# A two-layer network on one core: producers and consumers of layer 0 set one turn further apart, and the first entry into layer 1 held until the last scan

## The chip, the cores and the metric

The kernel runs on one core of a Trainium2 chip. The metric is the device time of one execution in microseconds (us), lower being better; the time of a kernel is the median of its runs. Before the change the median of three runs is 2766.09 us, from 2762.88 to 2768.23.

Five engines take part. TensorE (PE) multiplies matrices into PSUM, VectorE (DVE) does elementwise work and scans, ScalarE (ACT) does activations and copies, GpSimd (POOL) does some elementwise work and gathers, and SyncE (SP) issues transfers. Each works through its own instructions in order and waits on semaphores of the others.

## The reference, cut to what matters

The input x has 8 batch entries of 512 tokens of 256 channels, all in fp32. Each of two layers adds an attention-like part and a mixture of experts (MoE) to x, both computed from a layer norm of x. The first layer's attention is a linear recurrence along the tokens, run forwards and backwards:

```python
# layer 0, cut; xn = layernorm(x), per head K = 16 channels
dx  = conv(xn) - xn                                  # taps t-1, t, t+1
xxx = xn + dx * maa_x
m   = tanh(xxx @ maa_w1) projected by maa_w2, five ways
r, k, v, g = (mixed inputs) @ Wr, Wk, Wv, silu(@ Wg)
w_log = -exp(time_decay + tanh(xw @ decay_w1) @ decay_w2)
# forward:  S = exp(w_t) * S + k_t v_t^T ;  y_t  = r_t S
# backward: y_t += r_t S ;  S = exp(w_t) * (S + k_t v_t^T)
y = y * sigmoid(dx @ gate_w + gate_b)
x = x + (groupnorm(y) * ln_w + ln_b) * g @ Wo        # attention
      + sum over top 2 of 8 experts: score * W3(silu(xn W1) * (xn W2))
```

The second layer takes the layer norm of that x and adds a global latent attention followed by a local attention (window of 64), and an MoE with the top 4 of 16 experts and a shared part.

## The kernel before

Layer 0 comes first for all eight entries, then layer 1.

The order on PE, DVE, ACT and SP is the order in which the Python code emits instructions; these queues are pinned. The code is written as generators that yield at the end of a step. `Turns.turn()` advances every running generator by one step. So a `yield` in a generator is a distance of one turn in every pinned queue: what follows it stands behind whatever the other generators emit in that turn. This is the whole schedule: which engine waits for which is set by how many turns lie between a producer and its consumer.

`scans` sets the pace. It has 128 items, 8 entries b by 2 halves of the channels c by 8 groups of value channels vg, and each item has four turns. In the first turn DVE multiplies a tile kv by the keys (`L884`), and SP issues the eight transfers that fetch the next item's kv (`spread`, `L861`) into one of four buffers. Turns two and three each hold a pair of scans over the 512 tokens (`L895`, `L899`). In the fourth DVE multiplies by r (`L904`). What PE has to add up from the finished kv tiles (`sums`, `L910`) is kept in a list `late`, and emitted for two items at a time in the first turn of every second item. One entry b is thus 16 items or 64 turns.

Beside `scans`, these generators run:

- `projections(b + 1)` makes the next entry's inputs in three generators. `inputs` makes dx and xxx on DVE (`L748`, `L753`) and their projection t on PE (`L761`). `values` makes the gate, the values v, which go through memory (`vd`, `L782`) to `spread`, and the keys. `decays` makes the decay d (ACT, `L815`), q (DVE, `L819`), `near` (ACT, `L827`) and dq (DVE, `L831`). Its mixed inputs xf come from matmuls m (`L720`) and DVE (`L727`).
- `ending(b, c, ...)` follows the last sums of a half: gate yg (DVE, `L930`), centering yc (PE, `L933`), square and copy (ACT), variance (PE, `L943`), its root (ACT) and reciprocal (DVE, `L951`), widening (ACT, `L954`), transposes rs (PE, `L959`), scaling z (DVE, `L961`), and after the second half the output projection o (PE, `L973`), added to x on DVE (`L978`) and stored to `after`.
- `experts` works through 39 chunks of 256 token slots of the MoE in 12 turns each: a transposed input xsT (PE into PSUM, copied by ACT at `L598`), matmuls g and u (`L606`), silu, products h on DVE (`L615`), matmuls y (`L645`), and a store to `outs`.

After the last chunk, `last` starts `begin`. It loads layer 1's weights from ACT's queue and starts `entry(0)`, which gathers the experts' rows of entry 0 (POOL, `L286`), accumulates them on DVE (`L294`), normalizes, transposes and routes for layer 1.

PSUM banks are shared by tags; `rs` and `var` have the tag `rw`, whose two banks also serve some of the projections.

Of the kernel before, what the change touches and what calls it, by code (L numbers as in the profile page):

```python
# [26 lines left out]
F32 = mybir.dt.float32  # L27
I32 = mybir.dt.int32
AF = mybir.ActivationFunctionType
ALU = mybir.AluOpType  # L30
# [6 lines left out]
P = 128  # L37
B, T, D = 8, 512, 256
NC = D // P
NT = T // P  # L40
# [7 lines left out]
CH = 256  # L48
NS = CH // P
TOP0 = 2  # L50
NCH = B * T * TOP0 // CH + E0 - 1
# [114 lines left out]
def two_layers(ctx: ExitStack, tc: tile.TileContext, a: dict, out: bass.AP):  # L166
# [97 lines left out]
    done = set()  # L264

    def until(*what):
        while what not in done:
            yield
# [4 lines left out]
    def entry(b):  # L273
# [5 lines left out]
        nc.sync.dma_start(acc, tokens(after[b]))  # L279
        for half in range(2):  # L280
            ys = []
            for t in range(2 * half, 2 * half + 2):
                n = b * NT + t
                for i in range(2):
                    y = temp([P, D], "y0", f"y0_{n}_{i}", 4)
                    pool_e.indirect_dma_start(  # L286
                        out=y, out_offset=None, in_=outs,
                        in_offset=bass.IndirectOffsetOnAxis(ap=slot[i][:, n : n + 1], axis=0),
                    )
                    ys.append((t, n, i, y))  # L290
            yield
            yield
            for t, n, i, y in ys:
                vec_e.scalar_tensor_tensor(  # L294
                    acc[:, t, :], y, wslot[i][:, n : n + 1], acc[:, t, :], ALU.mult, ALU.add
                )
        yield
# [14 lines left out]
        ps = bank(f"lg_{b}")  # L312
# [54 lines left out]
    with ExitStack() as l0:  # L367
# [219 lines left out]
        def experts():  # L587
            nxt = weights(0, "wgu", a["w0_gu"], GU0, 2)
            xs = load_slots(0)
            for _ in range(3):  # L590
                yield
            ps = turned(0, xs)
            yield
            for i in range(NCH):
                w, xps = nxt, ps
                wd = weights(i, "wdn", a["w0_dn"], DN0, 1)
                xT = ex.tile([P, NC, CH], F32, tag="xT", name=f"xsT_{i}", bufs=1)
                act_e.copy(xT, xps)  # L598
                if i + 1 < NCH:
                    nxt = weights(i + 1, "wgu", a["w0_gu"], GU0, 2)  # L600
                    xs = load_slots(i + 1)
                yield

# [17 lines left out]
                for j in range(3):  # L621
                    g = ps_gu.tile([P, 2, CH], F32, tag="gu", name=f"g_{i}_{j}")
                    hidden(g[:, 0, :], 4 * j * D)
                    hidden(g[:, 1, :], (4 * j + 2) * D)
                    yield
                    if last:
                        product(j - 1, *last)
                    u = ps_gu.tile([P, 2, CH], F32, tag="gu", name=f"u_{i}_{j}")
                    n = 2 - j // 2
                    for k in range(n):  # L630
                        hidden(u[:, k, :], (4 * j + 2 * k + 1) * D)
                    act_e.activation(hs[j][:, :n, :], g[:, :n, :], AF.Silu)  # L632
                    if n == 1:
                        act_e.activation(hs[j][64:, 1, :], g[:64, 1, :], AF.Silu)
                    last = g, u
                    yield
                if i + 1 < NCH:
                    ps = turned(i + 1, xs)
                product(2, *last)
                yield  # L640
                y = ps_gu.tile([P, NS, D], F32, tag="gu", name=f"y_{i}")
                for n in range(NS):
                    for j in range(NJ0 + 1):
                        lo = 64 * (j == NJ0)
                        pe.matmul(  # L645
                            y[:, n, :], hs[j // 2][lo:, j % 2, n * P : (n + 1) * P],
                            wd[lo:, j * D : (j + 1) * D], start=j == 0, stop=j == NJ0,
                        )
                        if j % 3 == 2:
                            yield  # L650
                ys = ex.tile([P, NS, D], F32, tag="ys", name=f"ys_{i}", bufs=1)
                act_e.copy(ys, y)
# [7 lines left out]
        def projections(b):  # L660
# [75 lines left out]
            def inputs():  # L736
# [7 lines left out]
                for c in range(NC):  # L744
                    o = dx[:, c, :]
                    vec_e.tensor_scalar(o, xT[c], V("conv1", c), None, ALU.mult)
                    for s, n in ((-1, "conv0"), (1, "conv2")):
                        vec_e.scalar_tensor_tensor(o, shifted(c, s), V(n, c), o, ALU.mult, ALU.add)  # L748
                    yield
                xxx = []  # L750
                for c in range(NC):
                    t = mix(f"xxx{c}", c)
                    vec_e.scalar_tensor_tensor(t, dxs[c], V("maa_x", c), xT[c], ALU.mult, ALU.add)  # L753
                    xxx.append(t)
                yield
                both = ((t5a, 0, 0, P), (t5b, P, 64, 96))
# [35 lines left out]
            def decays():  # L792
# [22 lines left out]
                act_e.activation(dT, dT, AF.Exp, scale=-1.0)  # L815
                yield

# [8 lines left out]
                for c in range(NC):  # L826
                    act_e.activation(near[c], near[c], AF.Exp, scale=-1.0)  # L827
                yield
                dq = big("dq")
# [40 lines left out]
        def scans(turns):  # L870
# [4 lines left out]
            for n, (b, c, vg) in enumerate(todo):  # L875
# [8 lines left out]
                vec_e.tensor_tensor(kv, kv, bc(kc, 1, NV), ALU.mult)  # L884
                if len(late) == 2:
                    for sums in late:
                        sums()
                    late = []
                if vg == 0:
                    y = ps_s.tile([P, T], F32, tag="ys", name=f"ys{c}_{b}")  # L890
                if n + 1 < len(todo) and ("keys", todo[n + 1][0]) in done:
                    kvs[todo[n + 1]] = spread(*todo[n + 1])
                yield
                for i in range(NV):
                    vec_e.tensor_tensor_scan(  # L895
                        out=kv[:, i, :], data0=qc, data1=kv[:, i, :], initial=0.0,
                        op0=ALU.mult, op1=ALU.add,
                    )
                    vec_e.tensor_tensor_scan(  # L899
                        out=kv[:, i, ::-1], data0=dc[:, ::-1], data1=kv[:, i, ::-1],  # L900
                        initial=0.0, op0=ALU.mult, op1=ALU.add,
                    )
                    yield
                vec_e.tensor_tensor(kv, kv, bc(rc, 1, NV), ALU.mult)  # L904
# [12 lines left out]
                late.append(sums)  # L917
                yield
            for sums in late:
                sums()  # L920

        def ending(b, c, y, z, x):
# [7 lines left out]
            vec_e.tensor_tensor(yg, sig[:, c, :], y, ALU.mult)  # L930
            yield
            yc = ps_e.tile([P, T], F32, tag="e", name=f"yc{c}_{b}")
            pe.matmul(yc, C["center"], yg, start=True, stop=True)  # L933
# [3 lines left out]
            zc = z[:, c, :]  # L937
            act_e.copy(zc, yc)
            yield

# [13 lines left out]
            act_e.copy(wide, bc(sd, 2, HD))  # L954
            yield
            rs = ps_rw.tile([P, T], F32, tag="rw", name=f"rs{c}_{b}")
            for t in range(NT):
                cols = slice(t * P, (t + 1) * P)
                pe.transpose(rs[:, cols], wide[:, t, :, :].rearrange("p v h -> p (v h)"), ident)  # L959
            yield  # L960
            vec_e.tensor_tensor(zc, zc, rs, ALU.mult)  # L961
# [34 lines left out]
        def begin():  # L996
# [16 lines left out]
            turns.add(entry(0))  # L1013
            for _ in range(6):
                yield
            for name, of, shape in (
# [504 lines left out]
```

## Time and profile before

| | |
|---|---|
| median of 3 runs | 2766.09 us (2762.88 to 2768.23) |
| the profiled execution | 2771.45 us |
| its span in the profile | 2769.7 us |
| mean granted TensorE clock | 0.914 |
| PE busy | 2380.8 us, 86% |
| DVE busy | 2151.8 us, 78% |
| ACT busy | 882.4 us, 32% |
| POOL busy | 500.1 us, 18% |
| memory read, written | 215.22 MB, 31.46 MB |

The span is the time from the first to the last record of the profiled execution; its own time is 1.75 us longer. Busy shares are means over both layers and hide that their limits differ: layer 0 fills about the first 1500 us and layer 1 the rest. The views used below are the windows (busy time of every engine in stretches of time, with the granted PE clock), the waits (for each pair of a waiting line and the line it waited for: total, times, longest), and the groups of instructions by line (busy time, mean ns of one, idle time before them and what ended it).

### The profile page before, as it was taken

How to read it: one execution, taken by the hardware profiler on the slowest of the kernel's cores; microseconds unless marked ns; L12 is line 12 of the kernel's file. 1: busy time of each engine (PE TensorE's matmuls, PEld its weight loads, DVE VectorE, ACT ScalarE, POOL GpSimd, SP SyncE). 2: the span in 40 equal slices, each digit the busy share in tenths (PEclk: the TensorE clock that was granted, in tenths of full speed). 3: DMA queues.
4: the chain of work that ended last, by engine and by line, in shares of the span. 5: the costliest groups of instructions: out<-in, count | busy, mean ns of one | idle time of the engine just before them, and what ended most of it. 6: DMA issues, size and time to landing. Idle time of an engine off the chain costs nothing.

```text
span 2769.7 us, 32796 instructions
## 1 busy us (share of the span) xinstructions
PE 2380.8 (86%) x11900; PEld 1420.3 (51%) x11900; DVE 2151.8 (78%) x3063; ACT 882.4 (32%) x1684; POOL 500.1 (18%) x441
## 2 busy tenths in 40 slices
PE   6697998988989889798844899998989989998996
PEld 4354555545555555555622444555545545555554
DVE  7799989898898999989985766566676675656656
ACT  1232231222322223132111244434343433434344
POOL 2133222322323223232122100001010101001000
PEclk9689989999999899999965999999999999999998
DMA  6335445454454544554542100001011110000000
GB/s 220 106 97 151 140 132 173 141 147 131 146 155 149 149 149 141 158 151 135 157 137 85 45 22 24 12 24 29 19 32 31 31 31 29 24 22 26 20 9 16
DMA packets 100832, 248.87 MB, mean 90 GB/s; under 512 B 24992, under 2 KB 50368, under 8 KB 95552
## 3 DMA queue, kind: packets, MB, share of 16 engines
q1 hardware_dynamic: 70528, 113.32, 14.9%
q0 software_dynamic: 21168, 115.75, 13.2%
q10 hardware_dynamic: 8976, 17.69, 1.8%
q8 instruction: 96, 1.57, 0.2%
q14 instruction: 64, 0.52, 0.1%
HBM read 215.22 MB, written 31.46 MB: 89 GB/s over the span
## 4 chain that ended last, share of the span: by engine, by line
PE 55%; DVE 28%; issue 7%; DMA 4%; ACT 3%; SPq 2%; POOL 1%; DVEq 0%; ACTq 0%; POOLq 0%
PE y L1404 6%; PE g L1358 5%; PE u L1358 4%; DVE kv L895 4%; PE g L606 4%; PE y L645 4%; PE u L606 3%; DVE kv L899 3%; PE sc_g L1256 2%; DMA kv<-vd 2%; PE o_g L1284 2%; DVE kv L884 2%; PE ys L910 2%; PE t L761 2%; PE qkv_l L1148 2%
## 5 line engine op out<-in xcount | busy, mean ns | idle before, releaser
L899 DVE TENSOR_TENSOR_SCAN kv<-d,kv 128x512 f32<-128x512 f32 x256 | 336.5, 1314 | 8.8
L895 DVE TENSOR_TENSOR_SCAN kv<-dq,kv 128x512 f32<-128x512 f32 x256 | 321.6, 1256 | 2.6
L645 PE MATMUL y<-wdn,h 128*128 128x256 f32 x936 | 261.8, 419 | 12.1 <-DVE h L615 11.3
L606 PE MATMUL g<-xsT,wgu 128*128 128x256 f32 x936 | 236.7, 398 | 27.9 <-ACT xsT L598 24.2
L1264 ACT ACTIVATE pt_g<-sc_g 128x512 f32<-128x512 f32 (+1 forms) x384 | 171.0, 531 | 274.8 <-PE sc_g L1256 228.1
L645 PEld LDWEIGHTS y<-wdn,h 128*128 128x128 f32 x936 | 176.7, 203 | 112.8 <-issue 70.0
L606 PEld LDWEIGHTS g<-xsT,wgu 128*128 128x128 f32 x936 | 184.2, 200 | 87.1 <-ACT xsT L598 36.3
L1358 PE MATMUL g<-xT,w 128*128 128x512 f32 x384 | 205.5, 662 | 26.9 <-DVE att_l L1312 14.0
L910 PE MATMUL ys<-kv,cst 128*32 128x512 f32 x512 | 125.3, 685 | 96.3 <-DVE kv L904 96.1
L606 PE MATMUL u<-xsT,wgu 128*128 128x256 f32 x780 | 204.0, 403 | 0.0
L1358 PE MATMUL u<-xT,w 128*128 128x512 f32 x384 | 188.1, 612 | 10.7 <-ACT qkT_g L1216 6.0
L606 PEld LDWEIGHTS u<-xsT,wgu 128*128 128x128 f32 x780 | 150.8, 199 | 69.2 <-issue 42.7
L1404 PE MATMUL y<-w,h 128*128 128x256 f32 x768 | 183.6, 392 | 0.7 <-ACT qkT_g L1216 0.7
L632 ACT ACTIVATE h<-g 128x512 f32<-128x512 f32 (+1 forms) x117 | 61.2, 526 | 347.3 <-PE g L606 346.3
L884 DVE TENSOR_TENSOR kv<-kv,k 128x1024 f32<-128x1024 f32 x128 | 163.0, 1273 | 8.2 <-DMA kv<-vd 7.9
L904 DVE TENSOR_TENSOR kv<-kv,r 128x1024 f32<-128x1024 f32 x128 | 167.0, 1305 | 2.4
L1376 DVE TENSOR_TENSOR h<-h,u 128x512 f32<-128x512 f32 x96 | 66.0, 688 | 124.1 <-PE u L1358 114.5
L1404 PEld LDWEIGHTS y<-w,h 128*128 128x128 f32 x768 | 144.4, 194 | 34.3 <-issue 11.2
L730 POOL TENSOR_TENSOR xf<-xf,xnT 128x512 f32<-128x512 f32 x80 | 117.0, 1481 | 237.3 <-DVE xf L727 237.0
L1270 DVE TENSOR_TENSOR pt_g<-pt_g,cst 128x512 f32<-128x512 f32 x128 | 85.1, 686 | 75.1 <-ACT pt_g L1264 75.1
L1358 PEld LDWEIGHTS g<-xT,w 128*128 128x128 f32 x384 | 73.1, 202 | 113.2 <-issue 86.2
L1264 ACT ACTIVATE pt_l<-sc_l 128x384 f32<-128x384 f32 (+1 forms) x256 | 98.0, 469 | 86.4 <-PE sc_l L1256 69.1
(307 smaller groups left out, 3899.4 us busy)
## 6 DMA issues: line engine op xcount, KB each, us to landing
kv<-vd SPq DMA_DIRECT2D x1024, 64.0 KB
cb<-cd SPq DMA_DIRECT2D x128, 128.0 KB
outs<-ys POOLq DMA_DIRECT2D x39, 256.0 KB
w<-in_w ACTq DMA_DIRECT2D x12, 384.0 KB
xn<-in_x SPq DMA_DIRECT2D x8, 512.0 KB
xnT<-xT ACTq DMA_DIRECT2D x16, 256.0 KB
normed<-xn SPq DMA_DIRECT2D x8, 512.0 KB
xnT<-xnT SPq DMA_DIRECT2D x8, 512.0 KB
```

The source lines that it names most:

```text
L606: pe.matmul(o, w[:, at + c * P : at + (c + 1) * P], xT[:, c, :], start=c == 0, stop=c == NC - 1,)
L645: pe.matmul(y[:, n, :], hs[j // 2][lo:, j % 2, n * P : (n + 1) * P], wd[lo:, j * D : (j + 1) * D], start=j == 0, stop=j == NJ0,)
L730: pool_e.tensor_tensor(t, t, xT[c], ALU.add)
L884: vec_e.tensor_tensor(kv, kv, bc(kc, 1, NV), ALU.mult)
L895: vec_e.tensor_tensor_scan(out=kv[:, i, :], data0=qc, data1=kv[:, i, :], initial=0.0, op0=ALU.mult, op1=ALU.add,)
L899: vec_e.tensor_tensor_scan(out=kv[:, i, ::-1], data0=dc[:, ::-1], data1=kv[:, i, ::-1], initial=0.0, op0=ALU.mult, op1=ALU.add,)
L904: vec_e.tensor_tensor(kv, kv, bc(rc, 1, NV), ALU.mult)
L910: pe.matmul(y[r0 : r0 + 32, :], C["take"][:, 24 - 8 * at : 56 - 8 * at], kv[:, i, :], start=at == 0, stop=at == 3, skip_group_check=True,)
L1264: act_e.activation(pt[:, i, :end], scs[i][:, :end], AF.Exp, scale=0.25)
L1270: vec_e.tensor_tensor(pt[:, :, a0 : a0 + m], pt[:, :, a0 : a0 + m], bc(mask[:, :m], 1, 4), ALU.mult,)
L1358: pe.matmul(ps, w[:, k, c * P : (c + 1) * P], xT[:, c, :], start=c == 0, stop=c == NC - 1,)
L1404: pe.matmul(y[:, i, :], hs[k][:, (t + i) * P : (t + i + 1) * P], w1[j - 5 + k][:, 2, :], start=k == 0, stop=k == 5,)
```

## The change

Six places change.

1. `entry` gathers into tiles that hold both experts' rows of a token group, four groups at once for b=0 and two otherwise, and entry(0)'s arithmetic waits until `scans` is over.
2. `experts` copies xsT of the next chunk while the y matmuls of this one are under way, and emits each product one step later. A chunk still has 12 turns.
3. `inputs` gets one more turn ahead of xxx and one behind it; `decays` gets one more behind d and one behind `near`. The first entry does not.
4. `scans` emits the late sums behind the first pair of scans, one turn later than before.
5. `ending` gets one more turn behind yg, behind the square and copy, behind `wide` and behind the transposes rs.
6. `begin` loads the weights after the last `spread`, and no longer after six turns.

```diff
 def entry(b):
-        for half in range(2):
+        ahead = 2 if b else NT
+        for t0 in range(0, NT, ahead):
             ys = []
-            for t in range(2 * half, 2 * half + 2):
+            for t in range(t0, t0 + ahead):
+                y = temp([P, 2, D], "y0", f"y0_{b}_{t}", ahead)
                 n = b * NT + t
                 for i in range(2):
-                    y = temp([P, D], "y0", f"y0_{n}_{i}", 4)
...
             yield
             yield
-            for t, n, i, y in ys:
+            if b == 0:
+                yield from until("scans over")
+            for t, n, y in ys:
...
 def experts():
-            ps = turned(0, xs)
+            def copied(i, ps):
+                xT = ex.tile([P, NC, CH], F32, tag="xT", name=f"xsT_{i}", bufs=1)
+                act_e.copy(xT, ps)
+                xTs.append(xT)
+
+            copied(0, turned(0, xs))
             yield
             for i in range(NCH):
-                w, xps = nxt, ps
+                w, xT = nxt, xTs.pop()
...
-                act_e.copy(xT, xps)
...
-                yield
...
                     yield
-                    if last:
-                        product(j - 1, *last)
                     u = ps_gu.tile([P, 2, CH], F32, tag="gu", name=f"u_{i}_{j}")
...
+                    if last:
+                        product(j - 1, *last)
                     last = g, u
                     yield
                 if i + 1 < NCH:
                     ps = turned(i + 1, xs)
+                yield
                 product(2, *last)
                 yield
...
                         if j % 3 == 2:
                             yield
+                            if n + j == 2 and i + 1 < NCH:
+                                copied(i + 1, ps)
...
 def inputs():
+                for _ in range(0 if first else 1):
+                    yield
                 xxx = []
...
-                yield
+                for _ in range(1 if first else 2):
+                    yield
...
 def decays():
                 act_e.activation(dT, dT, AF.Exp, scale=-1.0)
-                yield
+                for _ in range(1 if first else 2):
+                    yield
...
                     act_e.activation(near[c], near[c], AF.Exp, scale=-1.0)
-                yield
+                for _ in range(1 if first else 2):
+                    yield
...
 def scans(turns):
                 vec_e.tensor_tensor(kv, kv, bc(kc, 1, NV), ALU.mult)
-                if len(late) == 2:
-                    for sums in late:
-                        sums()
-                    late = []
...
                     kvs[todo[n + 1]] = spread(*todo[n + 1])
+                if n + 1 == len(todo):
+                    done.add(("spread",))
                 yield
                 for i in range(NV):
...
+                    if i == 0 and len(late) == 2:
+                        for sums in late:
+                            sums()
+                        late = []
                     yield
...
+            done.add(("scans over",))
             for sums in late:
                 sums()
...
 def ending(b, c, y, z, x):
             vec_e.tensor_tensor(yg, sig[:, c, :], y, ALU.mult)
+            yield
             yield
...
             act_e.copy(zc, yc)
+            yield
             yield
...
             act_e.copy(wide, bc(sd, 2, HD))
             yield
+            yield
...
                 pe.transpose(rs[:, cols], wide[:, t, :, :].rearrange("p v h -> p (v h)"), ident)
+            yield
             yield
...
 def begin():
             turns.add(entry(0))
-            for _ in range(6):
-                yield
+            yield from until("spread")
```

More of the change, by code (lines that the diff above doesn't have):

```diff
@@ L279, in entry @@
         nc.sync.dma_start(acc, tokens(after[b]))
-        for half in range(2):
+        ahead = 2 if b else NT
+        for t0 in range(0, NT, ahead):
             ys = []
-            for t in range(2 * half, 2 * half + 2):
+            for t in range(t0, t0 + ahead):
+                y = temp([P, 2, D], "y0", f"y0_{b}_{t}", ahead)
                 n = b * NT + t
                 for i in range(2):
-                    y = temp([P, D], "y0", f"y0_{n}_{i}", 4)
                     pool_e.indirect_dma_start(
-                        out=y, out_offset=None, in_=outs,
+                        out=y[:, i, :], out_offset=None, in_=outs,
                         in_offset=bass.IndirectOffsetOnAxis(ap=slot[i][:, n : n + 1], axis=0),
                     )
-                    ys.append((t, n, i, y))
+                ys.append((t, n, y))
             yield
             yield
-            for t, n, i, y in ys:
-                vec_e.scalar_tensor_tensor(
-                    acc[:, t, :], y, wslot[i][:, n : n + 1], acc[:, t, :], ALU.mult, ALU.add
-                )
+            if b == 0:
+                yield from until("scans over")
+            for t, n, y in ys:
+                for i in range(2):
+                    vec_e.scalar_tensor_tensor(
+                        acc[:, t, :], y[:, i, :], wslot[i][:, n : n + 1], acc[:, t, :],
+                        ALU.mult, ALU.add,
+                    )
         yield
@@ L591, in experts @@
                 yield
-            ps = turned(0, xs)
+            xTs = []
+            def copied(i, ps):
[3 more added lines that the diff above has]
+            copied(0, turned(0, xs))
             yield
             for i in range(NCH):
-                w, xps = nxt, ps
+                w, xT = nxt, xTs.pop()
                 wd = weights(i, "wdn", a["w0_dn"], DN0, 1)
-                xT = ex.tile([P, NC, CH], F32, tag="xT", name=f"xsT_{i}", bufs=1)
-                act_e.copy(xT, xps)
                 if i + 1 < NCH:
```

## The prediction

> **What bounds it now.** I read the windows first, for the engine that is short in each stretch, then the waits of VectorE (DVE) and TensorE (PE), for what interrupts it, then the waits around the end of layer 0. The windows (DVE busy is the third figure after the width):
>
> ```profile
> core 0: us, PE busy (x) PEld busy (x) DVE busy (x) ACT busy (x) POOL busy (x), PEclk, DMA share, GB/s
> 400.00:600.00 200.00, 176.21 (x657) 108.45 (x656) 184.12 (x181) 52.15 (x81) 62.37 (x51) 0.93 0.49 148
> 600.00:800.00 200.00, 176.55 (x664) 110.55 (x665) 183.12 (x182) 48.28 (x77) 57.07 (x44) 0.91 0.50 147
> 1000.00:1200.00 200.00, 177.76 (x676) 108.57 (x674) 180.17 (x179) 52.55 (x81) 60.91 (x48) 0.94 0.48 142
> 1400.00:1450.00 50.00, 13.76 (x51) 5.21 (x50) 38.95 (x50) 3.88 (x6) 14.07 (x11) 0.59 0.50 138
> 1450.00:1500.00 50.00, 19.46 (x44) 7.51 (x42) 35.25 (x58) 3.83 (x6) 1.26 (x1) 0.53 0.26 82
> ```
>
> Two engines are each about 90% busy, neither full: they hand work to and fro in fixed order and wait in turns. Who waits for whom between 200 and 1300 us (total, times, longest), DVE's waits, then PE's:
>
> ```profile
> DVE h L615 <- PE u L606: 18.1, 12, 2.9
> DVE z L961 <- PE rs L959: 17.6, 8, 3.0
> DVE dq L831 <- ACT near L827: 14.4, 7, 2.2
> DVE x L978 <- PE o L973: 11.2, 10, 2.9
> DVE q L819 <- ACT d L815: 8.8, 7, 3.0
> DVE xf L727 <- PE m L720: 8.1, 8, 2.1
> ```
>
> ```profile
> PE ys L910 <- DVE kv L904: 37.0, 21, 3.8
> PE t L761 <- DVE xxx L753: 28.0, 6, 7.3
> PE g L606 <- ACT xsT L598: 21.7, 20, 1.2
> PE yc L933 <- DVE yg L930: 19.7, 7, 3.8
> ```
>
> A batch entry b is 16 items of four turns. Item 32's kv*k (L884) starts at 461.8, item 96's at 1148.3: 171.6 us per b. From 200 to 1200 us the windows hold 912.9 of DVE and 882.1 of PE per 1000: 156.7 and 151.4 per b. The six rows and a 0.5 left out here are 79 us in 1100, that is in 6.4 entries, 12.3 per b; so 159 is DVE's floor (its short gaps included), and a turn of DVE's work is 159/64 = 2.5 us. In the cycle of b=3 the order in time is: PE waits 7.0 at t L761 (649.7), while DVE has its heaviest item; then PE has more work than DVE for six items, and DVE waits 3.0 (z), 2.9 (x), 0.4, 0.5, 1.3 (h), 2.1 (xf), about 10 in all; then 0.9 and 2.2 for ScalarE (q, dq).
>
> The end of layer 0, 1390 to 1530 us:
>
> ```profile
> DVE kv L884 <- DMA kv<-vd: 7.9, 1, 7.9
> SPq L861 <- DMA w<-in_w: 31.7, 7, 25.1
> SPq L861 <- DMA rtw<-in_router_w: 12.7, 1, 12.7
> ```
>
> There DVE alone sets the pace, with entry(0)'s arithmetic between the last scans.
>
> **The change, part by part.** Instruction counts on PE, DVE, POOL and SP are equal; ACT has three table loads more. In turns from producer to consumer, the order moves these from 1 to 2: sums after kv*r (L910 after L904), t after xxx, q after d, dq after near, yc after yg, var after sq, rs after wide, z after rs, third product after u; xsT's copy to g from 1 to 3. xf after m, x after o, and yg after the sums stay at 1.
>
> *Steady state.* Relaxed DVE waits: z 17.6, dq 14.4, q 8.8, and the third product's share of the h row (its 128x256 form) 10.8: 51.6 us over 6.4 entries, 8.1 per b. They do not all go. The excess of PE's work over DVE's within a b, added up along the emitted order with the rows' means, reaches 17.5 us before and 17.0 after: the burst stays. What changes is how far the engines may part. PE may begin the burst one turn earlier (t and sums have a turn more): 2.5 us. On the other side DVE may run a turn further ahead at z, but x L978 and xf L727 stand at 1 and catch it: 0 to 2.5, taken as 0. The ScalarE waits, (14.4+8.8)/7 = 3.3, have a turn of 2.5 us against waits of 0.9 and 2.2 in b=3: 3.0. Sum 5.5 per b, between 0 and 8.1; over b=1 to 7, 38.5. In b=0 experts' first chunks gain the same waits for part of its length: 2.5.
>
> *Keys' transfers.* A spread of kv (L861, eight DMAs, 3.6 us to issue, landing 2.3 to 2.5 us after) reuses a buffer that the sums free. With the sums a turn later its lead over L884, mostly 10 to 30 us, falls by 2.5: free. Not so at item 6 of each b: SP's third DMA stands behind vd<-v landing, and vd<-v now goes out two turns (4.9 us) later, behind the new turns of `inputs`. The lead there is 5.7 us in two entries (L884 at 532.4 and 1048.1) and 9 to 11 in the others. If vd holds only the last DMAs, the cost is nothing; if it shifts the whole spread and DVE comes 5.5 earlier, 2 x (4.9+5.5+2.4-5.7) = 14 plus 5 x 2.3 = 12, or 26. I take 3 (1.5 in the two tight entries), since most of the eight issue ahead of it by the order.
> After<-x passes one spread of eight on SP in each b: 3.6 us on a queue that mostly waits; nobody needs `after` before layer 1.
>
> *Later endings.* The four added turns on each half of `ending`, and those of `inputs` and `decays`, add no instruction; what follows them starts up to four turns later in the same b. Cover is the length of a b, 64 turns; without it the next entry's keys would be late, which the transfers above price.
>
> *Gathers* of entry: the same indirect DMAs of the same bytes, all eight at once for b=0, beside the scans: 0, since the accumulations now wait longer for something else. In layer 1 two tiles hold what four held: 0.
>
> *xsT's copy* removes PE waits of 21.7 us, but PE is not short outside the burst; y's first matmul follows the copy in 10 of 30 chunks at under 1.2 us each. Counted in the burst, not again.
>
> *ACT tables.* The nearest row:
>
> ```profile
> L949 ACT ACT_TABLE_LOAD x16 | 20.5, 1283 | 0.3
> L825 ACT ACT_TABLE_LOAD x8 | 10.3, 1283 | 8.2 <-DVE q L820 7.7 <-ACT v L780 0.4
> ```
>
> At 1283 ns, with next to nothing idle before it but what it waits for, three make 3.8 us, on an engine a third busy. The Trainium skill ("ScalarE: Activation LUTs", What ACT_TABLE_LOAD costs) adds a drain of about 1380 ns, 2.66 us a switch: 8.0 us, against the change if they fall in the d-near chain. By the row I count 0 (the new turn covers one load); by the page up to 8.0 comes off.
>
> *The clock.* At t L761 PE sits idle 7.0 us, and from 650 to 656 us the granted clock is 0.62, from 656 it is 1.00: 6 x 0.38 = 2.3 us lost in the burst's opening. The skill ("TensorE: Matmul & The Clock Gate", What's actually happening) says an idle window of about 3.4 us halves the clock. The wait should shrink to 7.0-2.5 = 4.5, still over it, so the sum keeps the loss; under 3.4 it would gain another 7 x 2.3 = 16. The same rule speaks against a serial tail; but the tail shows 0.53 to 0.59 already, so 0 there by the row.
>
> *Tail.* From item 120's L884 (1390.4) to the scans' end (1484.1) are 93.7 us. Eight items at 7.36 (two multiplies, four scans) are 58.9, and h and ending operations 3.8: 62.7. The rest, 31.0, goes: entry(0)'s arithmetic 21.5 (eight accumulations of 0.48 are 3.9, statistics 2.4, norm 1.4, routing's one-hot and rank steps 13.8), the 7.9 above (SP held because kv's semaphores are shared with weight loads of `begin`, which now wait for the last spread), gathers 1.4. But entry(0)'s chain now runs after the scans, between yg and z of ending(7). From the scans' end to after<-x were 20.85; now these 21.5 come first on DVE, in its pinned order, with about 8.3 of trips between them (the last sums and yg 2.7, and POOL, PE and ACT for norm, transposes and scores, from the gaps that the same instructions show before), 29.8 in all, and z to after<-x 10.9 as before: 40.7, +19.9. Net -11.1. Unknown: from -31 (all beside ending's waits) to +10 (each hand-over a few us longer, weights late: 5.5 MB at the 138 GB/s of that window take 40 us from the last spread).
>
> Sum: -38.5 - 2.5 + 3 - 11.1 = -49 us. The profiled execution is 2771.45 us (span 2769.7 and 1.75 around it), 5.4 above the median of 2766.09. So 2722.4 on its basis and **2717** for the median. About 0.2% (5.5 us) is what a measurement of this kernel can tell from no change.
>
> **Rivals.**
> *A, main case*, 0.55: as above, 2700 to 2733.
> *B, all relaxed waits go*, 0.13: 8.1 x 7 = 57, clock 16, tail 11: 2766-84 = 2682. For it: PE's relief of over 100 us in the rows; against it: the two edges left at 1 and the unchanged 17 us excess.
> *C, the burst keeps DVE waiting*, 0.20: z's wait moves to x L978 and xf L727; only the ScalarE part of a few b's and the tail stay, 5 + 11: 2750. For it: x and xf wait 19.3 us already.
> *D, slower: lock-step at a PSUM bank*, 0.12. `rs` keeps one of the two rw banks a turn longer, and m L720 now waits for z L961 at distance 0 (twice per b), while xf L727 waits for m at 1. If DVE is the later one there, PE loses up to a turn (2.5) and then DVE up to 2.1 at xf: 4.6 twice, 9.2 per b, 64 in seven. Against the -52 of the other terms: +12, 2778. It decides above 3.7 us a meeting. Against it: in that stretch DVE waits for PE, so z is early.
> That the change does nothing is excluded: the order shows the distances moved.
>
> **Numbers.** Faster: A, B and 0.17 of C, 0.85; within 0.2%: 0.05; slower 0.10. The range leaves out D and the ends of B and C: 2680 to 2757.
>
> **What would show it.** L961, L819 and L831 nearly gone from DVE's waits; L978 and L727 not smaller; DVE near 189 of 200 us in the windows; a b of about 166 us; L884 waiting under 3 us in all; scans' end to layer 1 longer by 20 us. It is wrong if a b stays at 171, if m L720 waits for z, or if L884 waits for DMA at item 6.

## The result and the profile after

The changed kernel takes 2727.9 us in the median (2726.91 to 2730.55, four runs), the kernel before 2767.16 in the same comparison: a ratio of 0.9861, 95% interval 0.9843 to 0.9878, or 39 us less. The forecast was 2717. The profiled execution has a span of 2726.8 us, 42.9 less than before.

The windows of the changed kernel, with the columns as before:

```profile
400.00:600.00 200.00, 171.68 (x651) 106.17 (x650) 185.04 (x181) 50.58 (x78) 60.91 (x51) 0.93 0.50 149
...
1000.00:1200.00 200.00, 178.89 (x689) 108.88 (x690) 185.73 (x185) 50.35 (x79) 61.46 (x51) 0.96 0.53 157
...
1400.00:1450.00 50.00, 18.47 (x54) 8.72 (x54) 41.80 (x72) 5.94 (x9) 1.05 (x1) 0.50 0.21 69
1450.00:1500.00 50.00, 38.45 (x109) 19.81 (x110) 27.15 (x54) 11.80 (x21) 18.53 (x20) 0.82 0.30 88
```

DVE is busy for 941.8 of the 1000 us from 200 to 1200 (912.9 before); the two 50 us rows show layer 1 beginning about 40 us earlier. DVE's waits between 200 and 1300 us, all four of them, then PE's largest three and a smaller one that matters below (lines are some 10 to 25 further down: xf is L739, m L732, h L624, z L985, x L1002, kv*k L901, kv*r L923, sums L929):

```profile
DVE xf L739 <- PE m L732: 32.7, 10, 6.3
DVE h L624 <- PE u L615: 7.4, 6, 1.8
DVE z L985 <- PE rs L982: 0.9, 2, 0.6
DVE x L1002 <- PE o L997: 0.2, 1, 0.2
```

```profile
PE y L655 <- DVE h L624: 45.2, 24, 5.1
PE ys L929 <- DVE kv L923: 20.0, 9, 3.9
PE t L776 <- DVE xxx L767: 12.8, 4, 4.0
PE sig L697 <- ACT sig L791: 5.4, 2, 2.7
```

DVE's waits add up to 41 us where they were 79. Those for q and dq are gone, those for z and x nearly so (0.9 and 0.2), and a new one has grown from 8 to 33: xf waits for m. PE's waits for the sums, t and yc have shrunk; a wait for h has grown from 10.6 to 45.

What an entry b takes, from the kv*k of its first item to that of the next entry's, read off the starts of this instruction in each trace (us; "undone" is the changed kernel with that part as before, "alone" the kernel before with that part only):

| kernel | b=0 | 1 | 2 | 3 | 4 | 5 | 6 | scans' end | from there to the end |
|---|---|---|---|---|---|---|---|---|---|
| before | 193.2 | 171.7 | 170.2 | 173.4 | 171.9 | 171.1 | 172.7 | 1484.0 | 1285.6 |
| changed | 186.1 | 161.2 | 173.5 | 166.2 | 162.7 | 173.2 | 166.4 | 1423.7 | 1303.1 |
| endings undone | 187.3 | 165.3 | 168.9 | 162.1 | 167.5 | 168.6 | 162.1 | 1416.3 | 1301.2 |
| experts undone | 185.7 | 163.8 | 163.6 | 167.1 | 165.6 | 162.1 | 167.2 | 1409.7 | 1303.2 |
| rs in another bank | 186.9 | 160.9 | 170.2 | 165.6 | 162.3 | 170.4 | 166.1 | 1417.9 | 1305.8 |
| chunks a turn later | 187.0 | 161.1 | 166.4 | 168.1 | 163.5 | 166.6 | 168.2 | 1414.8 | 1301.9 |
| sums undone | 189.6 | 175.0 | 172.9 | 173.2 | 173.7 | 172.0 | 173.2 | 1470.3 | 1302.3 |
| inputs, decays undone | 192.5 | 173.5 | 175.3 | 176.3 | 174.1 | 175.3 | 176.3 | 1477.8 | 1300.2 |
| sums alone | 194.1 | 173.0 | 170.1 | 167.2 | 174.7 | 170.1 | 167.1 | 1475.0 | 1285.8 |
| inputs, decays alone | 184.3 | 170.8 | 164.1 | 171.0 | 170.4 | 164.1 | 170.8 | 1456.1 | 1285.0 |

In the changed kernel b=1 and 4 gain 10 us and b=2 and 5 lose 2 to 3. The pattern repeats every three entries because 16 chunks of 12 turns are three entries of 64 turns.

Each row is one profiled execution, and not always a typical one: that of "endings undone" took 2719.26 us where the other three of this kernel took 2728.12 to 2730.65, and some others lie 3 to 5 us from their medians. A difference of a few us in one row is not evidence by itself.

### The profile page after: what moved, and what is told of

Its sections match the earlier page's. It is cut to its first block, busy times and chain, and to the rows that moved or that the text cites. A ratio compares the mean times of both kernels' runs of the same rounds, so it can differ in the third digit from the quotient of the medians.

```text
span 2726.8 us, 32763 instructions
## 1 busy us (share of the span) xinstructions
PE 2362.4 (87%) x11900; PEld 1412.8 (52%) x11900; DVE 2157.0 (79%) x3063; ACT 888.3 (33%) x1687; POOL 477.5 (18%) x441
## 4 chain that ended last, share of the span: by engine, by line
PE 57%; DVE 25%; DMA 6%; issue 6%; ACT 2%; SPq 2%; POOL 1%; DVEq 0%; ACTq 0%; POOLq 0%
PE y L1427 6%; PE y L655 6%; PE g L1381 5%; DMA kv<-vd 5%; PE g L615 4%; PE u L1381 4%; PE u L615 4%; DVE kv L910 3%; PE sc_g L1279 2%; DVE kv L901 2%; PE ys L929 2%; PE o_g L1307 2%; DVE kv L914 2%; PE qkv_l L1171 2%; SPq L878 2%
## 5 line engine op out<-in xcount | busy, mean ns | idle before, releaser
L655 PE MATMUL y<-wdn,h 128*128 128x256 f32 x936 | 286.6, 443 | 54.9 <-DVE h L624 50.5
L615 PE MATMUL g<-xsT,wgu 128*128 128x256 f32 x936 | 229.2, 388 | 4.7 <-ACT h L639 3.2
L615 PEld LDWEIGHTS g<-xsT,wgu 128*128 128x128 f32 x936 | 176.1, 192 | 57.4 <-issue 27.4
L615 PE MATMUL u<-xsT,wgu 128*128 128x256 f32 x780 | 196.3, 392 | 0.0
L901 DVE TENSOR_TENSOR kv<-kv,k 128x1024 f32<-128x1024 f32 x128 | 172.0, 1344 | 6.6 <-DMA kv<-vd 6.6
L923 DVE TENSOR_TENSOR kv<-kv,r 128x1024 f32<-128x1024 f32 x128 | 162.9, 1273 | 3.6
L929 PE MATMUL ys<-kv,cst 128*32 128x512 f32 x512 | 105.7, 701 | 65.4 <-DVE kv L923 65.1
L1427 PEld LDWEIGHTS y<-w,h 128*128 128x128 f32 x768 | 144.4, 193 | 34.2 <-issue 11.2
L639 ACT ACTIVATE h<-g 128x512 f32<-128x512 f32 (+1 forms) x117 | 61.7, 527 | 272.6 <-PE g L615 262.5
```

Source lines behind the costliest of these rows:

```text
L615: pe.matmul(o, w[:, at + c * P : at + (c + 1) * P], xT[:, c, :], start=c == 0, stop=c == NC - 1,)
L655: pe.matmul(y[:, n, :], hs[j // 2][lo:, j % 2, n * P : (n + 1) * P], wd[lo:, j * D : (j + 1) * D], start=j == 0, stop=j == NJ0,)
L929: pe.matmul(y[r0 : r0 + 32, :], C["take"][:, 24 - 8 * at : 56 - 8 * at], kv[:, i, :], start=at == 0, stop=at == 3, skip_group_check=True,)
L1427: pe.matmul(y[:, i, :], hs[k][:, (t + i) * P : (t + i + 1) * P], w1[j - 5 + k][:, 2, :], start=k == 0, stop=k == 5,)
```

## The experiments

Each was timed beside the kernel before, and ratios are to that; a gain over the kernel before in us is worked out from the ratio. Gaps to the changed kernel are differences of medians.

**The end of layer 0 undone.** The changed kernel with these lines as before:

```diff
-        ahead = 2 if b else NT
+        for half in range(2):          # gathers of two groups, no wait for the scans
...
-            yield from until("spread")
+            for _ in range(6):
+                yield
```

> The changed kernel with entry(0)'s wait for the scans, its four-group gathers and begin's wait for the last spread undone. Theory (the end of layer 0 gains a little): in the two traces item 120 to the scans' end fell from 93.7 to 68.7 us, and the scans' end to layer 1 grew by 17.4, so the tail is worth 7.6 us and undoing it gives 2728 + 8 = 2736. Rival 1 (the tail gives it all back): 2728. Rival 2 (all of the 25 us counts, and what comes after is hidden in layer 1): 2753.

Measured: 2731.76 us, ratio 0.9869 (0.9854 to 0.9884). In its profile the entries are as in the changed kernel to 0.1 us; from item 120 to the scans' end are 89.8 us in place of 68.7, and from there to the end 1285.4 in place of 1303.1. The scans finish 21 us earlier by the change and 17.7 are given back, so 3.4 are left, and the medians differ by 4. Rival 2 is out; 8 was too much. By the times alone rival 1 is not out (2729.43 to 2732.56 us here, 2726.91 to 2730.55 in the changed kernel): that a few us are left rests on the two traces.

**Endings undone.** The changed kernel with the four added `yield`s of `ending` removed:

```diff
             vec_e.tensor_tensor(yg, sig[:, c, :], y, ALU.mult)
             yield
-            yield
...
```

> The changed kernel with only the four added turns of `ending` undone. Theory (the added turns let z and yc wait less, but rs now sits in one of the two rw banks between the two sig projections, and the second sig waits for ScalarE to read the first): z's waits of 2.7 us a b come back (+17 in all), and the two slow entries b=2 and b=5 (173 us against 161 to 166) lose theirs (-6 to -10 each, -16): 2729, no change, with a different pattern by entry. Rival (the added turns are the main gain of the change): 2728 + 17 = 2745. Rival 2 (they only do harm): 2712.

Measured: 2728.27 us, ratio 0.9862 (0.9847 to 0.9877): no change, as the theory said. But the way is not the one expected. The profiled execution is the 9 us shorter one, so its row of the table cannot be set against the changed kernel's by a few us. DVE's waits in it, 200 to 1300 us:

```profile
DVE x L998 <- PE o L993: 14.1, 7, 3.9
DVE kv L901 <- DMA kv<-vd: 11.6, 4, 3.5
DVE xf L739 <- PE m L732: 7.0, 2, 3.5
DVE h L624 <- PE u L615: 5.2, 4, 2.1
DVE q L835 <- ACT d L830: 1.1, 2, 0.6
```

z's wait for rs does not return with the turn taken away, neither here nor in a second version without it ("Both together" below). The row of the kernel before, 17.6 us at z, was therefore not paid for by the distance at z; it was where PE's lateness happened to be met.

**Experts undone.** The changed kernel with `experts` as before (copy, products and their turns).

> The changed kernel with `experts` as before. Theory (PE's waits for xsT and DVE's for the third product are real losses near the bound): they return, 21.7 + 10.8 us in 1100, and PE's new waits for h ahead of y (45 us) go; as DVE is the bound, only the 10.8 of DVE counts fully: 2728 + 12 = 2740. Rival (the new waits for h cost more than the old): 2715. Second rival (neither matters): 2728.

Measured: 2716.23 us, ratio 0.9816 (0.9803 to 0.9829), below the interval of the changed kernel. So this part of the change costs about 12 us, all of it before the scans' end (1409.7 against 1423.7) and most in b=2 and 5. The theory is refuted, and the rival has the size. What in the part costs it is asked by three more runs; its early copy of xsT was not undone alone.

**The third product one turn earlier.** The changed kernel with h a turn further ahead of y:

```diff
                     ps = turned(i + 1, xs)
-                yield
                 product(2, *last)
                 yield
+                yield
```

> The changed kernel with the third product of each chunk one turn earlier, right behind the transposes and two turns ahead of y; the early copy of xsT and the other products as in the change. Theory (what the experts part costs is h reaching y's matmuls only one turn after it is emitted, PE's 45 us of waits for h): those fall by half or more, and the kernel gains the 12 us that undoing the whole experts part gave: 2716. Rival (the cost is the place of the chunks against the burst, or the early copy): 2728. If u's wait comes back at the third product (1.7 us a b before), 2735.

Measured: 2744.53 us, ratio 0.9923 (0.9909 to 0.9938): 17 us slower than the changed kernel. Its waits, DVE's first:

```profile
DVE xf L739 <- PE m L732: 24.8, 6, 6.3
DVE h L624 <- PE u L615: 19.2, 11, 2.8
```

```profile
PE ys L929 <- DVE kv L923: 50.2, 21, 4.1
PE y L655 <- DVE h L624: 7.7, 10, 2.4
```

PE's 45 us of waiting for h fall to 8, and the time rises: the theory is refuted. DVE's waits for u come back (7.4 to 19.2), and PE waits longer for the sums (20.0 to 50.2). How long PE waits for h says little about the time: it is 32.3 us with the experts undone (2716 us), 48.9 with the chunks one turn later (2721 us), and 10.6 in the kernel before (2767 us). Where the 17 us come from is not settled. This edit takes the distance from u to the third product back to one turn, and it also moves that product a turn earlier against the scans. The distance alone is not enough: it is one turn with the experts undone too, and that kernel is 28 us faster than this one.

**Chunks one turn later.** The changed kernel with one empty turn ahead of the first chunk:

```diff
-            for _ in range(3):
+            for _ in range(4):
                 yield
             xTs = []
```

> The changed kernel with one empty turn more ahead of the first chunk of `experts`: every chunk stands one turn later against the entries, nothing else changes. Undoing the experts part gave 2716 and took b=2 and b=5 from 173 to 163 us. Theory A (it was the place of the chunks against the burst, which the experts part moved by a turn): b=2 and b=5 fall to about 165, in all 2714. Theory B (it is what the experts part does inside a chunk, h for y a turn later): the slow entries stay or only change places, 2728.

Measured: 2721.32 us, ratio 0.9839 (0.9823 to 0.9856). b=2 and 5 fall from 173 to 166.5, as theory A says, and b=3 and 6 rise by 2. The intervals overlap, but the runs do not (2718.43 to 2723.12 us against 2726.91 to 2730.55). An empty turn at the front changes the place of the chunks and nothing else, so about half of what the experts part seemed to cost (6.6 of 11.7 us) is their place against the entries. PE's two waits of sig for ScalarE, 5.4 us in the changed kernel, are not in this trace's list either: part of this gain is the pause that the next run takes away in another way.

**rs in another bank.** The changed kernel with

```diff
-            rs = ps_rw.tile([P, T], F32, tag="rw", name=f"rs{c}_{b}")
+            rs = ps_e.tile([P, T], F32, tag="e", name=f"rs{c}_{b}")
```

> The changed kernel with the transposes rs in the bank of yc and o (tag e) and no longer in the two rw banks; the order of instructions is the same. Theory (rs between the two sig projections makes the second wait for ScalarE, PE loses 2.7 us and then its clock, and DVE 4.7 to 6.3 at xf): the waits of sig for ScalarE's sig go, entries b=2 and b=5 come down from 173 to about 166 us, 14 us in all: 2714. Rival (DVE waits at xf because PE has more work in that stretch, whatever the bank): the waits stay or move on, 2728.

Measured: 2721.62 us, ratio 0.9833 (0.982 to 0.9847). Here is the place in the changed kernel's trace, b=2 (start, duration, engine, line; in brackets the idle time before and its cause), PE then DVE:

```profile
484.53 2.94 PE L697 MATMUL sig<-dx,wmix 128*128 128x512 f32 x4 [2.69 <-ACT sig L791]
487.27 2.66 PE L615 MATMUL u<-xsT,wgu 128*128 128x256 f32 x8
489.86 1.13 PE L732 MATMUL m<-t5a,m2a 32*128 32x512 f32 x4
```

```profile
491.02 1.41 DVE L739 SCALAR_TENSOR_TENSOR xf<-m,vecs,dx 128x512 f32<-128x512 f32 x2 [6.33 <-PE m L732]
```

The second sig projection needs the bank of the first, since rs has taken the other, and waits 2.69 us for ScalarE to read it. ScalarE is not idle meanwhile: it works off a silu of `experts`, the load of another table, and then the sigmoid that frees the bank:

```profile
481.88 0.60 ACT L639 ACTIVATE h<-g 128x512 f32<-128x512 f32 x1 [4.29 <-PE g L615]
482.49 1.28 ACT L791 ACT_TABLE_LOAD   x1
483.79 0.69 ACT L791 ACTIVATE sig<-sig,vecs 128x512 f32<-128x512 f32 x1
```

After the pause sig takes 2.94 us where the same four matmuls took 1.88 at 477.8, and the granted clock is 0.57 from 485 to 488 us. m comes late, and DVE waits 6.33. With rs in the other bank the waits of sig for ScalarE leave the list, sig takes 1.88 us both times, and the clock stays up in that stretch (the windows' row, PEclk 1.00):

```profile
485.00:490.00 5.00, 5.00 (x21) 2.64 (x20) 3.32 (x5) 2.56 (x4) 2.33 (x2) 1.00 0.01 3
```

b=2 and 5 come down by 3 each, 6 us in all where 14 were expected. DVE's wait at xf is still 24.2 us, so the bank is one cause of it and not the main one.

**Sums undone, and inputs and decays undone.** The changed kernel with the late sums back in the first turn:

```diff
-                    if i == 0 and len(late) == 2:
...
+                if len(late) == 2:          # ahead of the first yield of an item
+                    for sums in late:
+                        sums()
```

> The changed kernel with the late sums back in the first turn of an item. Theory (the sums' turn lets PE begin its burst earlier): PE's waits for kv*r come back (20 to about 37 us in 1100), half of them, 1.3 us per b, reach DVE: 2728 + 9 = 2737. Rival (PE is not short outside the burst, and the sums a turn earlier free kv's buffers earlier): 2728 or, with the kv wait of 6.6 us gone, 2721.

Measured: 2769.58 us, ratio 1.0014 (1.0006 to 1.0023). And with the added turns of `inputs` and `decays` removed:

```diff
-                for _ in range(1 if first else 2):
-                    yield
+                yield
...
```

> The changed kernel with `inputs` and `decays` without their added turns. Theory (the waits of DVE for ScalarE at q and dq, 23 us in 1100, are real, and PE's at t halve with the turn): they come back, 3.3 + 1 per b over seven: 2728 + 30 = 2758. Rival 1 (DVE's slack elsewhere absorbs them, as PE's work in the burst sets the pace): 2728 to 2735. Rival 2 (the keys come two turns earlier, and item 6's transfers are off the path): 2720.

Measured: 2785.01 us, ratio 1.007 (1.0055 to 1.0086). Each of these two, taken away, costs more than the whole change gains: 42 and 57 us against 39. Both expectations had the direction of their first theory and were far too small. The waits with the sums undone, DVE then PE:

```profile
DVE xf L739 <- PE m L732: 29.2, 10, 6.8
DVE yg L950 <- PE ys L929: 17.4, 8, 5.6
DVE z L985 <- PE rs L982: 14.3, 6, 4.0
DVE kv L901 <- DMA kv<-vd: 12.7, 3, 6.6
```

```profile
PE ys L929 <- DVE kv L923: 61.2, 28, 6.8
```

PE waits 61 us for kv*r ahead of the sums, and then DVE waits for what PE had behind them: yg, z, xf.

**Each alone, on the kernel before.**

> The kernel before with the sums' turn alone. Undoing it in the changed kernel cost 41 us. Theory (the turns hold only together: the pace of a b is set by the tightest of several loops between PE and DVE, and one left tight keeps it): 2760 to 2767. Rival (the parts add, the sums' turn is the gain of the change): 2767 - 41 = 2726.

Measured: 2761.61 us, ratio 0.998 (0.9971 to 0.9988): 5.5 us, as the theory said.

> The kernel before with the added turns of `inputs` and `decays` alone. Undoing them in the changed kernel cost 57 us. Theory (the turns hold only together): 2755 to 2767; DVE's waits for ScalarE at q and dq are gone (23 us in 1100) and come back as waits for PE. Rival (these turns are the gain): 2767 - 57 = 2710, or by the two rows alone 2767 - 23 = 2744.

Measured: 2747.58 us, ratio 0.9937 (0.9921 to 0.9952): 17 us, more than the theory's range allows, near the rival's 2744 and three quarters of the 23 that the rows of q and dq held, seven times each. They are gone from DVE's waits, and z's wait with them; part comes back as a wait for PE at x, 31.0 us where it was 11.2:

```profile
DVE x L983 <- PE o L978: 31.0, 12, 3.8
```

`inputs` and `decays` were not taken apart, so how much of this belongs to q and dq and how much to t stays open. Here is what PE is left waiting for, its first two lines in each, with the sums alone and then with the projections alone:

```profile
PE yc L936 <- DVE yg L933: 55.2, 9, 8.9
PE t L761 <- DVE xxx L753: 23.4, 6, 5.4
```

```profile
PE ys L915 <- DVE kv L909: 44.4, 21, 3.1
PE var L948 <- ACT sq L941: 29.1, 7, 6.3
```

With the sums alone, PE is stopped at yc and t; with the projections alone, at the sums.

These two runs also say what "undone" above did not. "Sums undone" is "inputs and decays alone" plus the parts in `ending`, in `experts` and at the end of layer 0, and by the ratios it is about 21 us slower; "inputs and decays undone" is "sums alone" plus the same parts, and about 25 us slower. So while one of the two sets of turns is missing, those parts together do harm (which of them is not shown), and the 42 and 57 us are not what one set of turns is worth.

**Both together, endings and experts as before.**

> The changed kernel with both `experts` and `ending` as before: what is left is the sums' turn, the turns of `inputs` and `decays`, and the end of layer 0. Undoing the endings alone changed nothing (2728), undoing the experts part alone gave 2716. Theory (the sums' turn and the projections' turns together carry the gain, the endings' turns nothing): 2716. Rival (the endings' turns are needed once the experts part is gone, since z then waits for rs again, 2.7 us a b): 2716 + 19 = 2735.

Measured: 2719.95 us, ratio 0.9845 (0.9827 to 0.9863). The sums' turn, the projections' turns and the end of layer 0 make 43 us; 5.5 + 17.4 + 4 would be 27. So the two together are worth about 16 us more than the sum of each alone (the intervals leave some 7 us either way), and the change gains nothing from `ending` and `experts` together: without them the kernel is no slower. Whether the endings' turns help once the experts part is gone is not clear: with them 2716.23 us, without 2719.95, and the intervals meet. The 19 of the rival are not there. The first two of DVE's waits:

```profile
DVE kv L894 <- DMA kv<-vd: 13.7, 3, 4.9
DVE x L991 <- PE o L986: 13.6, 10, 2.5
```

z does not appear in the list here either, and the keys' transfers have become the first wait.

**A version put together.**

> A version put together from the results: the changed kernel with `experts` as before, rs in the bank of yc and o, the last half's `ending` without its added turns, and begin's three small loads after the last spread. If the parts add: 2716 (experts undone) - 6 (bank) - 7 (the wait of item 123 for kv, held behind the small loads) - 8 (z of the last ending ahead of routing's long steps, its waits for o filled) = 2695. Rival (they hide the same waits): 2712. The tail alone is then 62 us from item 120 to the scans' end, and 1295 after it; if the small loads now come too late for entry(0), the rest grows by up to 10.

Measured: 2713.25 us, ratio 0.9804 (0.9788 to 0.9821), the fastest here, but its interval overlaps that of the kernel with only the experts undone (2716.23). The rival has it. The parts do not add: with the chunks where they were, b=2 and 5 are fast already and the bank has nothing to give. At the end of layer 0 neither edit helped. Two of DVE's waits from 1320 to 1480 us:

```profile
DVE kv L894 <- DMA kv<-vd: 7.2, 1, 7.2
DVE xg_g L1143 <- DMA cd<-cT: 4.2, 1, 4.2
```

The wait of item 123 for kv stays although the code emits the three small loads behind the last spread. The trace shows why: that order binds each queue only in itself. ACT issued the small loads at 1357 to 1358 us, when SP still had its last four spreads before it, and item 123's spread was held for the first of them, cstr:

```profile
SPq L871 <- DMA cstr<-in_cst: 13.8, 1, 13.8
1357.17 0.35 ACTq L1034 DMA_DIRECT2D cstr<-in_cst  x1
1366.86 18.79 SPq L871 DMA_DIRECT2D kv<-vd  x32
```

Layer 1 begins when cd is written, the last step of entry(0)'s own chain, where the changed kernel waits for after<-x (4.1). The two chains end at nearly the same time; shortening one changed nothing (1303.4 us to the end against 1303.1).

## Why the prediction came out as it did

**The sum.** It gave -49 on the profiled executions; measured are -42.9 on the spans. By its terms, from the table:

- *Steady state*, -38.5 for b=1 to 7: measured -27.8 for b=1 to 6 and -1.5 for b=7 up to item 120, so -29.3, or 4.6 per full entry where 5.5 were forecast; with the experts part undone it is 6.9. (The first item starts 1.0 later.) The floor of 159 was nearly reached in two entries (161.2, 162.7).
- *b=0*, -2.5: measured -7.1.
- *Keys' transfers*, +3: no wait of DVE for kv between 200 and 1300 us, so 0. The lead at item 6 fell from 5.7 to 2.6 us in the two tight entries, which just covers a landing of 2.3 to 2.5. In five of the other versions (endings undone, sums undone, chunks a turn later, projections alone, both together) 11.6 to 14.3 us of this wait do appear. The danger was rightly seen. That it did not show in the changed kernel may be owed to the 6.3 us that DVE loses at xf in item 3 of the tight entries, since item 6 comes that much later; with the chunks one turn later xf's wait is 20 us smaller and the wait for kv is 11.9. That is argued, not shown.
- *Tail*, -31.0 and +19.9: measured -24.9 and +17.5. The step that failed is "the 7.9 above" with its remedy, the weight loads that "now wait for the last spread": 6.6 of the wait for kv remain. SP is still held there, 11.0 us for cstr, one of three small loads that the change left where they were, and 3.9 for go, one of the weights. And in time the weights do not wait: ACT issued them from 1372.9 us, SP its last four spreads from 1381.7. The changed kernel's waits of DVE from 1340 to 1410 us, of SP from 1300 to 1500, and the two issues:

```profile
DVE kv L901 <- DMA kv<-vd: 6.6, 1, 6.6
SPq L878 <- DMA cstr<-in_cst: 11.0, 1, 11.0
SPq L878 <- DMA go<-in_g_wo: 3.9, 1, 3.9
1372.87 0.34 ACTq L1044 DMA_DIRECT2D gq<-in_g_wq  x1
1381.68 18.49 SPq L878 DMA_DIRECT2D kv<-vd  x32
```

The misses partly cancel: b=0 and the keys came out 7.6 us better than forecast, the steady state, the tail and the start 13.9 worse. That the sum came within 6 us is in part luck.

**What PE's lead needs.** The step "PE may begin the burst one turn earlier (t and sums have a turn more)" fits the runs, and they show the two sets of turns as the heart of the change: PE can only run ahead as far as its tightest wait for DVE allows, so t without the sums (17 us, with q and dq in it) and the sums without t (5.5 us) leave the other as the stop, while both together give about 16 more. The prediction counted this gain once per entry and did not say how far it hangs on having both, nor that the other parts do harm while one is missing.

**z.** That its relaxed wait would be "caught" at x and xf was right in kind. It was caught at xf alone (8.1 to 32.7 us), not at x, whose wait vanished too; and the turn at z was not what removed it: with the projections' turns alone it is gone too. The sign "L978 and L727 not smaller" was half wrong.

**The experts part** was reckoned to cost and gain nothing of its own. This is the wrong step of the sum with the largest effect: about 12 us lost. The table places most of them in b=2 and 5. About half is the place of the chunks, and some is rs's bank; the two runs on it (7 and 6 us) were not combined, both take away the same pause at sig, and what else is in it stays open. Rival D named the bank, but for m L720 behind z; measured is its neighbour, sig behind ScalarE.

**ACT tables.** Three loads more at the same 1283 ns each (27 for 25 at silu, L639, 4 for 2 at tanh, L783, 3 for 4 at L865). q and dq do not wait for ScalarE any more. Of the drain of about 1380 ns that the Trainium skill ("ScalarE: Activation LUTs", What ACT_TABLE_LOAD costs) adds to each switch, nothing is seen: in the lines of the bank's run above the load starts 0.01 us after the silu ends, and the sigmoid 0.02 us after the load.

**The clock.** The mean granted clock went from 0.914 to 0.916, so putting this term at 0 was right. Its reason was not: the prediction took the idle window of about 3.4 us that the Trainium skill states ("TensorE: Matmul & The Clock Gate", What's actually happening) as the shortest pause that costs clock. The trace before already has a shorter one, PE's wait for xxx in b=4, with the 3 us behind it granted 0.50:

```profile
821.62 3.62 PE L761 MATMUL t<-xxx,m1w 128*128 128x512 f32 x4 [2.83 <-DVE xxx L753]
822.00:825.00 3.00, 3.00 (x4) 1.01 (x3) 2.96 (x5) 0.62 (x1) 0.00 (x0) 0.50 0.00 0
```

After the change t's four waits are 2.4 or 4.0 us, the clock beside each of them is 0.50, and so it is behind the 2.69 us at sig. So a wait shrunk to under 3.4 us would not have brought the 16 us of rival B.

Of the rivals, B did not come (41 us of DVE's waits remain), C came in part, as the wait at xf, and D's price was paid at sig, twice between 200 and 1300 us and at 2.7 us each.

## What to carry to other kernels

Where two engines pass work back and forth in fixed order, each can run ahead only as far as the smallest distance over all the places where it waits for the other. Relax those places together: one set alone gave 5.5 us here, another 17, both about 39, and parts that cost little beside both cost over 20 us while one was missing. So undoing one part of a change does not measure that part's worth.

The row of waits says where a late engine is met and not which distance made it late: taking most of PE's 45 us for h away gained nothing, and z's 17.6 us were not z's. Every added turn also shifts what stands beside it: try the phase of a periodic helper by an empty turn before judging a rearrangement of its inside. And an order of emission holds back nothing in another queue: a load that is to come after another queue's transfers would have to wait for something they signal (not tried here).

## What was not expected of the hardware

DVE's elementwise work took up to three times as long where POOL did some at the same time: kv*k of 1024 elements took 3.72 us at 495.86 while POOL worked on xf (496.34, 2.15 us), against 1.22 us at 475.10 with no elementwise work on POOL.

```profile
475.10 1.22 DVE L901 TENSOR_TENSOR kv<-kv,k 128x1024 f32<-128x1024 f32 x1
...
495.86 3.72 DVE L901 TENSOR_TENSOR kv<-kv,k 128x1024 f32<-128x1024 f32 x1
496.34 2.15 POOL L742 TENSOR_TENSOR xf<-xf,xnT 128x512 f32<-128x512 f32 x2
```

The trace of the changed kernel has it throughout: the 118 of the 128 kv*k that no elementwise instruction of POOL overlaps took 1.21 to 1.23 us each, the ten that one overlaps took 1.84 to 3.80. Over the whole kernel kv*k took 172.0 us after the change and 163.0 before, and kv*r 162.9 and 167.0: which of the two meets POOL is a matter of turns as well. No run took POOL's work away, so that POOL is the cause is argued from this coincidence, not shown.
